# Block transposes on VectorE and row-placing DMAs in place of PE transposes, in a two-layer attention kernel

## The chip, the cores and the metric

The kernel runs on one core of one Trainium2 chip. The metric is device time in microseconds (us). The engines are PE (TensorE: matmuls, with weight loads of their own as PEld), DVE (VectorE), ACT (ScalarE), POOL (GpSimd) and SP (SyncE), which here issues every DMA. Each engine works through its own queue in order. PE writes to PSUM[...].

## The reference

Four batches of 512 tokens with 320 features go through two layers. Each layer is a self-attention, a cross-attention to a context of 1601 rows of 192 features, and a gated feed-forward with inner width 1280. All is fp32. There are 20 heads of 16 features. Cut to what matters:

```python
def _attn(x, ctx, wq, wk, wv, wo, bo, heads):
    ...
    sim = jnp.einsum('bhid,bhjd->bhij', q, k) * scale
    a = jax.nn.softmax(sim, axis=-1)
    out = jnp.einsum('bhij,bhjd->bhid', a, v)
    out = out.transpose(0, 2, 1, 3).reshape(b, n, heads * dh)
    return out @ wo + bo
h1 = _ln(x, n1_g, n1_b)
x = _attn(h1, h1, q1, k1, v1, o1_w, o1_b, heads) + x
h2 = _ln(x, n2_g, n2_b)
x = _attn(h2, context, q2, k2, v2, o2_w, o2_b, heads) + x
h3 = _ln(x, n3_g, n3_b)
proj = h3 @ ff_w1 + ff_b1
a, g = jnp.split(proj, 2, axis=-1)
return a * jax.nn.gelu(g, approximate=False) @ ff_w2 + ff_b2 + x
```

The softmax of a query needs the maximum of its scores, and at the end a division by the sum of its exponentials.

## The kernel before

**Units.** Attention is cut into units of one batch and four heads: per layer 20 units of self-attention (4 batches x 5 groups of heads), then 20 of cross-attention, then 4 feed-forward units, one per batch. A unit's keys are taken in chunks of 128: `nch` is 4 in a self unit and 13 in a cross unit (the last of 65 keys). `main` (L854) walks over the chunks of one unit. A chunk is two rounds; `tick` (L327) counts them in `clock["round"]`.

**Slots.** The four heads of a unit lie in slots of 32 partitions. 16 rows of a slot hold the head's features; the row `AUG` of the slot is a row of ones in the keys and a row of zeros in the queries. So that an exponential needs no bias, the negated maximum of each query is put into that row: the score matmul then subtracts it. Per chunk and head there is one score matmul (`st`, L862, queries moving, keys as weights), one exponential on ACT (`pr`, L868), and in `values` (L875), one chunk later, one matmul of the values (`av`, L882), with a column of ones for the sum of the exponentials. ACT copies the result from PSUM (`vo`, L898) and POOL adds it to `u.o` (L899), which holds the outputs with queries along the free axis, 16 rows and the row of sums (row `DH` of each slot).

**Maxima.** The maxima are found a unit ahead: beside every two score matmuls of unit n run two matmuls `sps` (L713) of a unit to come, with queries as weights and keys moving, and DVE reduces each of them (L721). `max_pairs` (L694) lists them, `giver` (L1079) hands them out so that they are done by a given number of rounds before that unit's start; a pair is at hand three rounds after the queries and keys that it reads were made. In a cross unit partial maxima `pm` are reduced once more by `max_reduce` (L758), one chunk before the end. They are queries on partitions. `max_end` (L764), after the scores of the last chunk, turns them: four transposes on PE (`mps`, L768), into PSUM, and one DVE addition of the queries `u.q` gives `qT` (L772), which the next unit's scores read.

**Finish.** `add_finish` (L774) is called when a unit's last values are emitted, in the first chunk of the next unit. `divide` (L777): four PE transposes of `u.o` (`dps`, L780), a reciprocal of the sums (L784), a product into `on` (L789). After the fifth group of heads `turn` (L796) transposes `on` back in three sets of four (`aps`, L801), with an ACT copy each into `aT` (L802), and eight steps of `project` (L804, `ops`) multiply by the output weights and add to `x`.

**Order.** The program order is written out by hand, and each engine keeps it. What stands beside the chunks (projections of queries and keys, values, context, norms, finish) waits in `chains`, as steps with a cost in us of PE time, a due round and conditions (`add`, L286). `steps` (L331) takes from them after each chunk, by due round (`pick`, L295) and by a credit that `pace` (L309) fills; steps of cost `LIGHT` have no PE work and are rationed to one or two per chunk. [...]a ring of four, `ps_st`, for scores and values, and a ring of four, `ps_m`, for the maxima and for the steps' matmuls (`step_bank`, L271). So a step or a maximum takes the bank that DVE or ACT has to leave first.

**DMAs.** `dma` (L80) is SP's `dma_start`. At the start `load_x`, `load_self`, `load_out`, `load_bias`, `load_cross` and `load_ff` (L1130 to L1138) are called before anything else; then the first unit's maxima are made without other units beside them, and `max_end(first)` (L1159) ends the start.

Of the kernel before, what the change touches and what calls it, by code (L numbers as in the profile page):

```python
# [59 lines left out]
def kernel(ctx: ExitStack, tc: tile.TileContext, x, context, ws, out):  # L60
# [51 lines left out]
    for i in range(2):  # L112
        m = const.tile([P, NQ, HG, SLOT], F32, name=f"nmax{i}")
        nc.gpsimd.memset(m, 0.0)
        nmax.append(m)
# [173 lines left out]
    def late_by(n):  # L289

        if clock["tiles"] is None or chains[n][0][0][0] == LIGHT:
            return 0
        return 0 if (n in ALIKE) == clock["tiles"] else 3
# [232 lines left out]
    held = {}  # L526
# [18 lines left out]
    def add_proj(u):  # L545
# [3 lines left out]
        due = lead(u) - 4  # L549
# [85 lines left out]

        for part in range(parts):
            add(chain, (0.05 + 0.427 / parts,) * 3, lambda part=part: queries(part), due - 2)
# [56 lines left out]
    def max_pairs(u):  # L694
# [4 lines left out]
        nm = nmax[u.n % 2]  # L699
# [10 lines left out]
        def full_one(t, s, j):  # L710
# [9 lines left out]
            to = nm[:, t, j, AUG[j] : AUG[j] + 1] if ns == 1 else u.pm[:, t, j, s : s + 1]  # L720
# [37 lines left out]
    def max_reduce(u):  # L758
        nm = nmax[u.n % 2]
        if u.pm is not None:  # L760
            for js in (slice(0, 2), slice(2, 4)):
                nc.vector.tensor_reduce(nm[:, :, js, AUG[js.start]], u.pm[:, :, js, :], AX.X, ALU.max, negate=True)

    def max_end(u):  # L764
        nm = nmax[u.n % 2]
        ps = step_bank([P, N], "mps")
        for t in range(NQ):
            nc.tensor.transpose(  # L768
                ps[:, t * P : (t + 1) * P], nm[:, t, :, :].rearrange("p j s -> p (j s)"), ident
            )  # L770
        u.qT = two.tile([P, N], F32, tag="qT", name="qT")
        nc.vector.tensor_tensor(u.qT, ps, u.q, ALU.add)  # L772

    def add_finish(u):  # L774


        def divide():  # L777
            ps = step_bank([P, NQ * HG, SLOT], "dps")
            for t in range(NQ):
                nc.tensor.transpose(  # L780
                    ps[:, t * HG : (t + 1) * HG, :].rearrange("p j s -> p (j s)"), u.o[:, t * P : (t + 1) * P], ident
                )
            rd = two.tile([P, NQ * HG], F32, tag="rd", name="rd")
            nc.vector.reciprocal(rd, ps[:, :, DH])  # L784
            if u.g == 0:
                held["out"] = one.tile([P, NQ, D], F32, tag="on", name="on")
            u.on = held["out"]
            u.divided = clock["round"]
            nc.vector.tensor_tensor(  # L789
                u.on[:, :, u.g * GD : (u.g + 1) * GD].rearrange("p t (j d) -> p t j d", d=DH),  # L790
                ps[:, :, :DH].rearrange("p (t j) d -> p t j d", j=HG),
                rd.rearrange("p (t j o) -> p t j o", j=HG, o=1).to_broadcast([P, NQ, HG, DH]),
                ALU.mult,
            )

        def turn(k, at, n):  # L796
            if k == 0:
                held["outT"] = one.tile([P, 3, N], F32, tag="aT", name="aT")
            ps = step_bank([P, N], "aps")
            for t in range(NQ):  # L800
                nc.tensor.transpose(ps[:n, t * P : (t + 1) * P], u.on[:, t, at : at + n], ident)  # L801
            nc.scalar.copy(held["outT"][:n, k, :], ps[:n, :])  # L802

        def project(t, part):  # L804
            cols = slice(part * D // 2, (part + 1) * D // 2)
            ps = step_bank([P, 512], "ops")
            for k, at, n in DK:
                for f, m in tiles_of(P):
                    nc.tensor.matmul(  # L809
                        ps[f : f + m, : D // 2],  # L810
                        lhsT=held["outT"][:n, k, t * P + f : t * P + f + m],
# [5 lines left out]

        r = clock["round"]
        add("divide", 0.58, divide, r + 6, yes, lambda: clock["round"] >= r + 2)
        if u.g == G - 1:  # L820
            for k, at, n in DK:
                add(
                    "divide", 0.58, lambda k=k, at=at, n=n: turn(k, at, n), r + 8 + k,
                    lambda: not chains["project"],
                    lambda: clock["round"] > u.divided,
                )

            def end():
                now = clock["round"]
                for t in range(NQ):  # L830
                    for part in range(2):
                        add(
                            "project", (0.317,) * 3, lambda t=t, part=part: project(t, part),
                            now + 6 + u.nch * t + u.nch // 2 * part,
                        )
                add("project", 0.0, lambda: after(u), now + 6 + u.nch * NQ)

            add("divide", 0.0, end, r + 10)
# [15 lines left out]
    def main(u, give, nxt):  # L854
# [3 lines left out]
        def score(c, j, pool=ps_st, tag="st"):  # L858
# [4 lines left out]
                st[:r, :], lhsT=u.kT[rows, u.k0 + c * P : u.k0 + c * P + r], rhs=u.qT[rows, :], start=True, stop=True  # L863
# [11 lines left out]
        def values(c):  # L875
# [15 lines left out]
            if c == 0:  # L891
                u.o = two.tile([P, N], F32, tag="o", name="o")
# [10 lines left out]
        for c in range(u.nch):  # L903
# [19 lines left out]
            if not last and c == u.nch - 1:  # L923
                max_end(nxt)
# [10 lines left out]
            if not last and c == u.nch - 2:  # L935
                max_reduce(nxt)
# [7 lines left out]
    def add_norms(i):  # L944

        while norms and norms[0].i <= i + (1 if norms[0].kind == "ff" else 5):
# [3 lines left out]
            else:  # L950
# [4 lines left out]
                due = lead(u) - 8  # L955
# [123 lines left out]
    def giver(u):  # L1079
# [14 lines left out]
        def give(h, alone=False):  # L1094
# [6 lines left out]
            for v in ahead:  # L1101
# [3 lines left out]
                rest = v.start - (7 if alone else 2) - clock["round"]  # L1105
# [5 lines left out]
            while owed >= 1.0 and any(left(v) for v in ahead) and not (alone and rounds and rest > -4):  # L1111
                hand = [v for v in ahead if left(v) and all(q and at_hand(v, q) for q in v.pairs)]
                if not hand and ahead[0].start - 2 - clock["round"] > 1:
                    break
# [92 lines left out]
```

## Time and profile before

| | |
|---|---|
| median of 3 runs | 3355.0 us (3354.72 to 3355.11) |
| profiled execution, its own time | 3355.09 us |
| its span, first to last instruction | 3353.3 us |
| granted TensorE clock | 0.999 |
| PE / DVE / ACT / POOL busy | 99 / 60 / 61 / 45% |
| four transposes `mps`, `dps` each, 80 times | 52.7 and 52.3 us busy |
| `aps`, 192 transposes in 48 sets | 29.4 us busy |
| ACT copies `aT`, 48 | 27.6 us busy |

A group's line names the kernel's line, the engine, what is written and read, and the count; then its busy time in us, the mean length of one in ns, and the idle time of the engine just ahead of it, with what ended it. Busy time is the union of the group's stretches; several matmuls on parts of the PE array run at once, so a group's busy time is less than count times mean. The ends of matmuls are modelled. A timeline line has the start and length in us. "SPq" is SP's queue: the time is that of issuing, and the landing is told apart. The self stages lie at about 30 to 435 and 1703 to 2110 us, the cross stages at 437 to 1400 and 2111 to 3066, the feed-forward between and after them.

### The profile page before, as it was taken

The page shows a single profiled execution, that of the slowest core. Times are in us where ns is not written, and L with a number is a line of the kernel's source. Part 1 is how long each engine was busy: PE and PEld are TensorE (multiplying, and loading weights), DVE is VectorE, ACT ScalarE, POOL GpSimd, SP SyncE. Part 2 cuts the span into 40 slices and gives each one's busy share as a digit, 9 for nine tenths or more (in the row PEclk, how much of TensorE's full clock was granted, in tenths as well). Part 3 has the DMA queues.
Part 4 walks back from the last instruction along what each step waited for, and adds up shares of the span by engine and source line. Part 5 has one row for each costly group of instructions (what it writes and reads, how often), then busy time and mean ns, then how long its engine had stood idle before and what let it go on. Part 6 is the DMA issues. An engine that isn't in the chain of part 4 may idle for free.

```text
span 3353.3 us, 81403 instructions
## 1 busy us (share of the span) xinstructions
PE 3315.3 (99%) x34386; PEld 1533.0 (46%) x34386; DVE 2025.8 (60%) x3724; ACT 2062.3 (61%) x4239; POOL 1519.6 (45%) x2252
## 2 busy tenths in 40 slices
PE   9999999999999999999999999999999999999999
PEld 4444444444444444355444444544444444443555
DVE  7666667767767666522256666677676676664221
ACT  5666467877877877711146664677777777776110
POOL 4544445645645654211225444456456556542000
PEclk9999999999999999999999999999999999999999
DMA  4001000100100000000020000000000000000000
GB/s 131 2 7 29 16 7 2 31 2 3 30 2 4 26 2 12 1 6 2 1 75 2 2 4 2 7 2 16 2 16 2 2 17 2 2 2 1 9 10 14
DMA packets 32117, 41.96 MB, mean 13 GB/s; under 512 B 11780, under 2 KB 30216, under 8 KB 30472
## 3 DMA queue, kind: packets, MB, share of 16 engines
q1 hardware_dynamic: 31752, 36.76, 3.9%
q8 instruction: 270, 4.42, 0.6%
q14 instruction: 95, 0.78, 0.1%
HBM read 29.21 MB, written 7.54 MB: 11 GB/s over the span
## 4 chain that ended last, share of the span: by engine, by line
PE 93%; DVE 5%; POOL 1%; ACT 1%; issue 1%; DMA 0%; SPq 0%; POOLq 0%; ACTq 0%; DVEq 0%
PE st L862 22%; PE av L882 19%; PE sps L713 15%; PE fps L984 8%; PE yps L1019 5%; PE kps L613 5%; PE vps L661 5%; PE ops L809 3%; PE qps L588 3%; PE fps L996 2%; DVE pm L721 2%; DVE nmax L721 2%; PE sps L728 2%; PE dps L780 1%; PE hps L422 1%; PE mps L768 1%
## 5 line engine op out<-in xcount | busy, mean ns | idle before, releaser
L868 ACT ACTIVATE pr<-st 128x512 f32<-128x512 f32 (+1 forms) x2720 | 1410.2, 601 | 559.9 <-PE sps L713 453.5
L721 DVE TENSOR_REDUCE pm<-sps 128x1 f32<-128x512 f32 x1920 | 1195.5, 683 | 498.3 <-PE sps L713 496.2
L862 PE MATMUL st<-qT,kT 32*128 32x512 f32 (+1 forms) x5440 | 1354.8, 614 | 22.1 <-DVE qT L772 10.1
L713 PE MATMUL sps<-kT,q 32*128 32x512 f32 x5120 | 1282.2, 617 | 2.3 <-ACT kst L630 1.5
L899 POOL TENSOR_TENSOR o<-o,vo 128x512 f32<-128x512 f32 x576 | 730.7, 1269 | 1124.2 <-ACT vo L898 1045.1
L882 PE MATMUL av<-pr,vals 128*32 128x512 f32 (+1 forms) x5440 | 729.3, 605 | 3.1 <-ACT pr L868 3.1
L862 PEld LDWEIGHTS st<-qT,kT 32*128 32x128 f32 (+1 forms) x5440 | 457.8, 181 | 275.5 <-ACT pr L868 96.4
L713 PEld LDWEIGHTS sps<-kT,q 32*128 32x128 f32 x5120 | 455.0, 183 | 243.6 <-issue 181.1
L721 DVE TENSOR_REDUCE nmax<-sps 128x1 f32<-128x512 f32 x640 | 397.0, 682 | 188.9 <-PE sps L713 188.0
L543 POOL TENSOR_SCALAR kT<-kst,keep,ones 64x200 f32<-64x200 f32 (+2 forms) x796 | 414.1, 520 | 88.9 <-ACT kst L623 31.5
L898 ACT COPY vo<-av 128x512 f32<-128x512 f32 x576 | 348.5, 605 | 47.6 <-PE av L882 47.2
L882 PEld LDWEIGHTS av<-pr,vals 128*32 128x32 f32 (+1 forms) x5440 | 109.8, 108 | 449.8 <-ACT pr L868 423.4
L984 PE MATMUL fps<-hT,w 128*128 128x512 f32 x640 | 288.2, 598 | 0.0
L1002 ACT ACTIVATE gl<-fps,b 128x512 f32<-128x512 f32 x80 | 54.8, 687 | 371.3 <-PE fps L996 371.3
L543 POOL TENSOR_SCALAR q<-qst,keep,zero 64x128 f32<-64x128 f32 (+1 forms) x476 | 230.0, 483 | 96.2 <-ACT qst L600 66.9
L984 PEld LDWEIGHTS fps<-hT,w 128*128 128x128 f32 x640 | 117.0, 190 | 141.7 <-issue 136.1
L661 PE MATMUL vps<-wv,ctxT 96*32 96x192 f32 (+2 forms) x3264 | 148.0, 299 | 0.0
L370 POOL TENSOR_SCALAR root<-root 128x4 f32<-128x4 f32 x23 | 5.3, 229 | 309.3 <-DVE root L364 308.8
L661 PEld LDWEIGHTS vps<-wv,ctxT 96*32 96x32 f32 (+1 forms) x3264 | 102.0, 109 | 94.3 <-issue 79.3
L669 ACT COPY vals<-vps 128x128 f32<-128x128 f32 (+3 forms) x272 | 82.4, 303 | 91.0 <-PE vps L661 87.4
L613 PE MATMUL kps<-ctxT,wk 96*32 96x200 f32 (+1 forms) x2560 | 136.9, 332 | 0.0
L1003 DVE SCALAR_TENSOR_TENSOR hid<-fps,b,gl 128x512 f32<-128x512 f32 x48 | 35.8, 750 | 155.1 <-ACT gl L1002 152.7
(83 smaller groups left out, 2465.6 us busy)
## 6 DMA issues: line engine op xcount, KB each, us to landing
ctxT<-ctxT SPq DMA_DIRECT2D x8, 1200.8 KB, 6.8
w<-in_L_xattn_ff_w_dram SPq DMA_DIRECT2D x4, 1280.0 KB, 9.2
ctxin<-in_ctx_dram SPq DMA_DIRECT2D x24, 192.0 KB, 2.6
w<-in_L_xattn_ff_w_dram SPq DMA_DIRECT2D x2, 1600.0 KB, 11.3
out_dram<-x SPq DMA_DIRECT2D x16, 160.0 KB, 1.8
x<-in_x_dram SPq DMA_DIRECT2D x3, 640.0 KB, 10.5
w1r<-in_L_xattn_ff_w_dram SPq DMA_DIRECT2D x4, 320.0 KB, 10.2
wq<-in_L_xattn_q_dram SPq DMA_DIRECT2D x8, 140.0 KB, 2.4
```

The lines of the kernel that those rows point to most:

```text
L543: nc.gpsimd.tensor_scalar(to, stage[rows, :w], keep[b][rows], more[rows], ALU.mult, ALU.add)
L613: nc.tensor.matmul(ps[to, :w], lhsT=wk[:n, k, gs], rhs=first.kvT[:n, k, c0 : c0 + w], start=(k == 0), stop=(k == len(u.kck) - 1),)
L661: nc.tensor.matmul(ps[f : f + m, at : at + w], lhsT=u.kvT[:n, k, c * P + f : c * P + f + m], rhs=wv[:n, k, h0 * DH : h1 * DH], start=(k == 0),
L713: nc.tensor.matmul(ps, lhsT=u.q[j * SLOT : (j + 1) * SLOT, t * P : (t + 1) * P], rhs=u.kT[j * SLOT : (j + 1) * SLOT, u.k0 + s * 512 : u.k0 ...
L721: return lambda: nc.vector.tensor_reduce(to, ps, AX.X, ALU.max, negate=(ns == 1))
L862: nc.tensor.matmul(st[:r, :], lhsT=u.kT[rows, u.k0 + c * P : u.k0 + c * P + r], rhs=u.qT[rows, :], start=True, stop=True)
L868: nc.scalar.activation(p[:r], st[:r], AF.Exp)
L882: nc.tensor.matmul(ps[i * SLOT : (i + 1) * SLOT, :], lhsT=columns_of[:r, head : head + SLOT], rhs=pr.pop((c, j))[:r, :], start=True, stop= ...
L898: nc.scalar.copy(vo, ps)
L899: nc.gpsimd.tensor_tensor(u.o, u.o, vo, ALU.add)
L984: nc.tensor.matmul(ps, lhsT=w1[:, k, i * FF + c * P : i * FF + (c + 1) * P], rhs=u.hT[:, k, :], start=(k == 0), stop=False,)
L1019: nc.tensor.matmul(ps[:, :D], lhsT=hid[c][:, t * P : (t + 1) * P], rhs=w2[:, c, :], start=(c == 0), stop=(c == NHC - 1),)
```

## The change

The maxima are written into 16 columns of a small tile `nm` [128, 32] in SBUF. `max_end` turns it on DVE as four squares of 32 by 32, so that each of 4 x 16 rows holds the maxima of 32 queries, and eight DMAs write these rows into the `AUG` rows of the queries `u.q` themselves: four for heads 0 and 1, four for heads 2 and 3, each of eight runs of 128 bytes. The scores read `u.q`; `qT` is gone. `max_reduce` and `max_end` are called one chunk earlier, and the maxima are due four rounds before a unit's start in place of two.

The finish is three steps: `sums` turns all 16 x 4 squares of `u.o` on DVE and takes the reciprocal, `divide` multiplies and turns back into `u.o`, and `turn` lets four DMAs put a unit's 4 x 16 rows into their place in `aT`. A projection comes at the earliest three rounds after the last `turn`. Since `u.q` is read by the scores until the unit ends, new queries wait until the unit that had the buffer is scored (`unread`). Queries, keys and norms are due two rounds sooner.

```diff
-        m = const.tile([P, NQ, HG, SLOT], F32, name=f"nmax{i}")
+        m = const.tile([P, SLOT], F32, name=f"nmax{i}")
...
-        if clock["tiles"] is None or chains[n][0][0][0] == LIGHT:
+        if clock["tiles"] is None or sum(chains[n][0][0]) < 0.1:
...
-        due = lead(u) - 4
+        due = lead(u) - 6
...
+        def unread():
+            return u.n < 3 or u.early or attn[u.n - 3].early or attn[u.n - 3].scored == attn[u.n - 3].nch
...
-            add(chain, (0.05 + 0.427 / parts,) * 3, lambda part=part: queries(part), due - 2)
+            add(chain, (0.05 + 0.427 / parts,) * 3, lambda part=part: queries(part), due - 2, unread)
...
     def max_reduce(u):
         if u.pm is not None:
-            for js in (slice(0, 2), slice(2, 4)):
-                nc.vector.tensor_reduce(nm[:, :, js, AUG[js.start]], u.pm[:, :, js, :], AX.X, ALU.max, negate=True)
+            nc.vector.tensor_reduce(
+                u.nm[:, : HG * NQ].rearrange("p (j t) -> p t j", t=NQ), u.pm, AX.X, ALU.max, negate=True
+            )

     def max_end(u):
-        ps = step_bank([P, N], "mps")
-        for t in range(NQ):
-            nc.tensor.transpose(
-                ps[:, t * P : (t + 1) * P], nm[:, t, :, :].rearrange("p j s -> p (j s)"), ident
-            )
-        u.qT = two.tile([P, N], F32, tag="qT", name="qT")
-        nc.vector.tensor_tensor(u.qT, ps, u.q, ALU.add)
+        turned = two.tile([P, SLOT], F32, tag="turned", name="turned")
+        nc.vector.transpose(turned, u.nm)
+        for half in range(2):
+            slots = u.q[half * GD : (half + 1) * GD, :].rearrange("(j s) n -> s j n", s=SLOT)[AUG[2 * half]]
+            for i in range(P // SLOT):
+                rows = slice(i * SLOT + half * 2 * NQ, i * SLOT + (half + 1) * 2 * NQ)
+                dma(
+                    out=slots.rearrange("j (t r) -> j t r", t=NQ)[:, :, i * SLOT : (i + 1) * SLOT],
+                    in_=turned[rows, :],
+                )
...
+        def sums():
+            nc.vector.transpose(turned.rearrange("p b s -> p (b s)"), u.o)
+            u.rd = two.tile([P, N // SLOT], F32, tag="rd", name="rd")
+            nc.vector.reciprocal(u.rd, turned[:, :, DH])
+            when.append(clock["round"])
+        def divide():
+            nc.vector.tensor_tensor(
+                turned[:, :, :DH], turned[:, :, :DH],
+                u.rd.rearrange("p (b o) -> p b o", o=1).to_broadcast([P, N // SLOT, DH]), ALU.mult,
+            )
+            nc.vector.transpose(u.o, turned.rearrange("p b s -> p (b s)"))
+            when.append(clock["round"])
+        def turn():
             if u.g == 0:
-                held["out"] = one.tile([P, NQ, D], F32, tag="on", name="on")
+                held["outT"] = two.tile([P, 3, N], F32, tag="aT", name="aT")
+            for j in range(HG):
+                f = u.g * GD + j * DH
+                k = next(k for k, at, n in DK if at <= f < at + n)
+                row = f - DK[k][1]
+                dma(out=held["outT"][row : row + DH, k, :], in_=u.o[j * SLOT : j * SLOT + DH, :])
+            if u.g == G - 1:
+                end(held["outT"])
...
-        add("divide", 0.58, divide, r + 6, yes, lambda: clock["round"] >= r + 2)
+        add("divide", LIGHT, sums, r - 20, yes, since(0, 2))
+        add("divide", LIGHT, divide, r - 20, yes, since(1, 1))
+        add("divide", 0.0, turn, r - 20, lambda: u.g or held["open"] < 2, since(2, 1))
...
-                rhs=u.qT[rows, :], start=True, stop=True
+                rhs=u.q[rows, :], start=True, stop=True
...
-                u.o = two.tile([P, N], F32, tag="o", name="o")
+                u.o = three.tile([P, N], F32, tag="o", name="o")
...
-            if not last and c == u.nch - 1:
+            if not last and c == u.nch - 2:
                 max_end(nxt)
...
-            if not last and c == u.nch - 2:
+            if not last and c == u.nch - 3:
                 max_reduce(nxt)
...
-                due = lead(u) - 8
+                due = lead(u) - 10
...
-                rest = v.start - (7 if alone else 2) - clock["round"]
+                rest = v.start - (7 if alone else 4) - clock["round"]
```

## The prediction

> **What bounds the kernel now.** I read the page's engine totals first, then the groups kept apart by form, then the timeline of one engine at a time around a boundary between two units. Columns of the first fence: busy us (share of the span) x instructions.
>
> ```profile
> PE 3315.3 (99%) x34386; PEld 1533.0 (46%) x34386; DVE 2025.8 (60%) x3724; ACT 2062.3 (61%) x4239; POOL 1519.6 (45%) x2252
> ```
>
> PE has 38 us of idle in 3353.3; no other engine is above 61%. So PE work that goes saves its own time, unless a new wait takes its place. The groups that the change removes (busy us, mean ns of one, idle before):
>
> ```profile
> L768 PE MATMUL mps<-ident,nmax 128*128 128x128 f32 x320 | 52.7, 287 | 0.3 <-DVE nmax L721 0.3
> L780 PE MATMUL dps<-ident,o 128*128 128x128 f32 x320 | 52.3, 286 | 2.6 <-POOL o L899 2.3 <-DVE pm L721 0.3
> L801 PE MATMUL aps<-ident,on 128*112 128x128 f32 x128 | 19.4, 282 | 0.0
> L772 DVE TENSOR_TENSOR qT<-mps,q 128x512 f32<-128x512 f32 x80 | 54.3, 679 | 6.8 <-PE mps L768 6.8
> ```
>
> Ends of matmuls are modelled, so I price a group of four transposes by starts. First an ordinary chunk of a cross unit, then the last chunk of one (PE timeline: start, length, what):
>
> ```profile
> 1007.42 0.70 PE L862 MATMUL st<-qT,kT 32*128 32x512 f32 x2
> ...
> 1009.35 1.07 PE L882 MATMUL av<-pr,vals 128*32 128x512 f32 x8
> 1010.23 0.86 PE L613 MATMUL kps<-ctxT,wk 96*32 96x200 f32 x16
> 1011.02 0.70 PE L862 MATMUL st<-qT,kT 32*128 32x512 f32 x2
> ```
>
> ```profile
> 1079.97 0.65 PE L862 MATMUL st<-qT,kT 32*65 32x512 f32 x2
> ...
> 1081.91 0.66 PE L768 MATMUL mps<-ident,nmax 128*128 128x128 f32 x4
> 1082.49 1.07 PE L882 MATMUL av<-pr,vals 128*32 128x512 f32 x8
> 1083.49 0.64 PE L501 MATMUL cps<-ident,ctxin 128*96 128x128 f32 x4
> 1084.39 0.70 PE L862 MATMUL st<-qT,kT 32*128 32x512 f32 x2 [0.25 <-DVE qT L772]
> ```
>
> Scores to values takes 1.93 us without mps and 2.52 with: a group costs 0.59. The ordinary chunk is 3.60 long, the boundary chunk 4.42: 0.59 of that is mps, the other 0.23 the wait for qT, which stands behind four reduces on DVE (2.48 us from 1081.16). Last, SP's queue at the start:
>
> ```profile
> 33.55 2.27 SPq L155 DMA_DIRECT2D w<-in_L_xattn_ff_w_dram  x2
> 35.86 1.11 SPq L199 DMA_DIRECT2D w1r<-in_L_xattn_ff_w_dram  x2
> 37.01 0.61 SPq L203 DMA_DIRECT2D w<-in_L_xattn_ff_w_dram  x1
> ```
>
> SP issues weights until 37.6 us, while PE starts its first scores at 30.27. In the DMA view of the first 40 us the last of these, 1600 KB, takes 15.0 us to land: 52.0.
>
> [...] No transpose of DVE is in this trace. [...] The additions from PSUM agree with such a rate: 160, 320 and 512 elements take 323, 492 and 679 ns, about 1 ns each plus 160. [...] Here the smallest loads (0.4 KB) land 2.0 us after issue, output stores 1.8.
>
> **The change part by part.** Price of a turn on DVE, not in the trace: 512 elements 0.69 us by the additions' line[...]. I take 0.69[...], and 0.2 for 32 elements.
>
> *Removed from PE:* mps and dps once in each of 80 units, aps three times in each of 16 batches and attentions: 208 groups x 0.59 = 122.7 us. With them go 48 ACT copies (27.6 us, off the path) and PSUM buffers that these shared with the maxima. The qT add goes too: its wait 0.23 x 38 cross boundaries = 9 us, and about 3 in the self stages: 12.
>
> *Added to DVE:* per unit two turns of 512 and one of 32 (1.58), against the qT add (0.68). Reciprocal (0.25) and product (0.42) stay; two reduces of 0.18 become one in a cross unit. Net some +0.8 us x 80 = 64 us on an engine at 60%. The finish comes as 0.94 (turn, reciprocal) in one chunk and 1.11 (product, turn) in the next. Behind them on DVE stand the next reduces, and for those PE waits, through the four PSUM buffers. What hides them is the idle between reduces: DVE works 2.48 of 3.60 us in an ordinary chunk, 1.1 free. Both fit; 5 us for coincidences with norm work. Without that cover they would cost their length.
>
> *Added to SP, maxima:* eight transfers of 1 KB per unit, four for heads 0 and 1, then four for heads 2 and 3. They are called one chunk before the old place. Clock from the start of chunk nch-2, cross stage: its last reduce ends at 3.44 in nearly all units, turn to 3.64, SP starts at 3.74. Issues in a row start 0.41 to 0.47 apart (four x loads in 1.81 us); at 0.46 the fourth is issued at 5.12 and the eighth at 6.96, and with 2.0 to land (range 1.6 to 2.4) they are there at 7.12 and 8.96. PE wants heads 0 and 1 at 3.64 + 3.60 = 7.24, so the first half is hidden, and heads 2 and 3 at 8.22 (0.98 into the chunk): 0.74 late. Four cross boundaries have longer chunks and room: 0.74 x 34 = 25. Self chunks are mostly 4.3 to 7 us: hidden except at a few dense boundaries, 8 in all. Behind the waiting score stand all of PE's matmuls, so a stall is paid in full.
>
> *Waits:* each half waits for four landings, up to eight more semaphore instructions of 0.05 us on PE's sequencer per unit (32 in all); most pass while matmuls run: 8.
>
> *Maxima due two rounds sooner, queries only once the unit three before is scored:* no work is added. In a self unit queries, keys and 16 maxima must now fit 12 rounds; I put it at 0, and the loss into the rivals' range.
>
> *Outputs:* four transfers per unit, 1.8 us of SP, with three rounds (6 us) before a projection reads them: hidden by that slack. SP in all: 12 x 80 x 0.46 = 442 us of 3353.
>
> *The start:* the first burst stands behind all start-up loads in SP's queue. Also, a transfer seems to wait for the one issued eight before it: x lands at 21.17 (9.2 after its issue at 11.97) and the eighth issue after it starts at 21.21; the next x lands at 22.94 and its eighth follower, a wq with nothing to do with x, starts at 22.97. Eight before the burst's last is the 1600 KB of w. So it starts at 52.0 and lands at 54.1; the scores of heads 2 and 3 of unit 0, at 31.2 before, wait for it: 23 us, with nothing else for PE. In mid-kernel the 1200 KB context transfers (6.8 us) may sit ahead of a burst once or twice: 5.
>
> Sum against the profiled span: 3353.3 - 122.7 - 12 + 23 + 25 + 8 + 8 + 5 + 5 = 3292.6. The profiled execution took 3355.09, 1.8 more than its span; the median of the three runs is 3355.0, so the same offset serves: 3294.
>
> **Rivals.** *All landings hidden.* If these transfers land in 1.6 us, the second half comes at 8.56 and the stall falls by more than half; with waits and coincidences at nothing I get 3250. For it: stores land in 1.8. Against: it needs every small term at its best.
>
> [...]
>
> *The burst on SP is dearer, and the kernel slower.* Some start-up issues took 0.6 us (w above, 0.61). At 0.65 an issue the eighth starts 1.33 us later: the cross stage stalls 2.1 at 34 boundaries, and about every self boundary by 0.9: 71 + 36 = 107 instead of 34, with the first half late too. That is 3368. It decides from about 0.61 us per issue, or as much in landing (3.1 us instead of 2.0).
>
> That the transposes stay is excluded: no line of mps, dps or aps is left; those of hps and cps are not touched.
>
> **How the numbers follow.** Forecast 0.52 (its own range 3265 to 3322), hidden 0.16, slow turns 0.16 (a fifth of it not faster), dearer burst 0.16. Faster by over 0.2% (6.7 us, about what this measurement can tell): 0.52 + 0.16 + 0.13 = 0.81; within 0.03; slower 0.16. The range 3243 to 3348 runs from the hidden case to the slow turns and leaves out most of the dearer burst.
>
> **What would show it.** Right: no mps, dps, aps on PE; PE's busy time near 3190; first scores of heads 2 and 3 near 54 us; PE idle before st released by DMA, 0.5 to 1 us at cross boundaries; turns of 0.69. Wrong: PE waiting on DVE's turns or reduces after a finish, starved maxima in the self stages, or bursts landing over 5.5 us after their turn.

## The result, and the profile after

The changed kernel takes 3387.8 us (median of 4 runs, 3386.79 to 3392.44) where the kernel before took 3354.86 (3353.26 to 3355.11): a ratio of 1.0102, 95% interval 1.0084 to 1.0119. It is slower by 33 us; the prediction was 3294 and its range ended at 3348. The profiled execution took 3392.44 us, its span is 3390.7, the granted clock 0.985 (0.999 before). It is the longest of the four, so the figures from its trace sum to 37 us more than before, not 33.

The page's engine totals of the kernel after:

```profile
PE 3263.5 (96%) x33554; PEld 1458.7 (43%) x33554; DVE 2092.3 (62%) x3844; ACT 2038.8 (60%) x4191; POOL 1526.0 (45%) x2252
```

832 transposes, 208 groups of four, are gone from PE, as the prediction counted (34386 - 33554), but its busy time fell by 52 us in place of 123, and its idle time rose from 38 to 127 us. The groups by form say what the new work on VectorE costs, and what PE waits for (columns as before):

```profile
L804 DVE STREAM_TRANSPOSE o<-oturn 128x512 f32<-128x512 f32 x80 | 56.9, 711 | 2.7
L794 DVE STREAM_TRANSPOSE oturn<-o 128x512 f32<-128x512 f32 x80 | 56.0, 701 | 25.9 <-POOL o L913 25.7
...
L772 DVE STREAM_TRANSPOSE turned<-nmax 128x32 f32<-128x32 f32 x80 | 16.1, 201 | 0.4 <-DVE nmax L764 0.4
```

```profile
L876 PE MATMUL st<-q,kT 32*128 32x512 f32 x5120 | 1315.2, 625 | 82.5 <-DMA q<-turned 55.1 <-ACT pr L882 12.6 <-DVE nmax L725 7.5
L717 PE MATMUL sps<-kT,q 32*128 32x512 f32 x5120 | 1305.4, 628 | 23.0 <-POOL kT L543 21.5 <-ACT kst L630 1.2 <-DVE kT L537 0.3
```

The turns are what was forecast (0.69 and 0.2 us). PE's new idle time has two names: the transfers into the queries' rows, 55.1 us (24.2 of them at the start), and POOL's writing of keys, 21.5 us, which is in no line of the kernel before. By stages, from the first scores of a stage to the first of its last unit or of the next stage; the forecast is the recorded sum split by where its groups and terms lie (of the 208 groups 96 lie in the self stages, 100 in the cross stages, 12 elsewhere; the small terms are halved):

| | before | after | forecast change | measured |
|---|---|---|---|---|
| start, to the first scores | 30.3 | 53.3 | +23 | +23 |
| self stages (two) | 406.9, 407.5 | 416.3, 412.6 | -43 | +15 |
| cross stages (two) | 933.5, 925.5 | 928.9, 935.9 | -34 | +6 |
| the rest | 649.8 | 643.7 | -6 | -6 |

So the start was right and both kinds of attention stage were off, by 57 and by 40 us.

**The start.** SP's queue and the first scores on PE:

```profile
37.77 0.59 SPq L203 DMA_DIRECT2D w<-in_L_xattn_ff_w_dram  x1
38.53 15.73 SPq L777 DMA_DIRECT2D q<-turned  x8
```

```profile
53.32 1.22 PE L876 MATMUL st<-q,kT 32*128 32x512 f32 x2 [24.24 <-DMA q<-turned]
```

The eight issues take 15.73 us. In the trace SP's transfers raise eight semaphores in turn, and the issue of the last one waits for the semaphore of the 1600 KB, issued eight before: those landed at 53.75 us, and it was issued at 53.77. But heads 0 and 1 waited nearly as long: their four transfers were issued by 45.2 us and landed only at 52.7 to 53.2, when the 1600 KB were nearly in.

**A cross boundary.** DVE, SP and PE around the start of the eleventh cross unit of layer 1 (start, length in us, what; in brackets idle before and its end):

```profile
2631.36 0.20 DVE L772 STREAM_TRANSPOSE turned<-nmax 128x32 f32<-128x32 f32 x1
```

```profile
2631.71 4.45 SPq L777 DMA_DIRECT2D q<-turned  x8
```

```profile
2635.06 0.70 PE L876 MATMUL st<-q,kT 32*128 32x512 f32 x2 [0.54 <-DMA q<-turned]
2635.07 0.70 PE L717 MATMUL sps<-kT,q 32*128 32x512 f32 x2
2635.57 0.62 PE L876 MATMUL st<-q,kT 32*128 32x512 f32 x2
2635.61 0.59 PE L717 MATMUL sps<-kT,q 32*128 32x512 f32 x2
2637.29 0.80 PE L876 MATMUL st<-q,kT 32*128 32x512 f32 x2 [1.09 <-ACT pr L882]
...
2637.82 1.12 PE L876 MATMUL st<-q,kT 32*128 32x512 f32 x2
...
2638.90 1.93 PE L896 MATMUL av<-pr,vals 65*32 65x512 f32 x8
```

Eight issues take 4.45 us, 0.56 each from start to start. PE waits 0.54 us for heads 0 and 1, and heads 2 and 3 start 2.23 us after them where 0.98 is the pace without a wait. (The bracket blames an exponential; but the last of the eight transfers landed at 2637.15, 0.14 us before these scores, and a run below shows that they can start without that exponential.) In 32 of 40 cross units this distance is over 1.5 us, mostly 2.1 to 2.3. After it the matmuls themselves are slow: values of 1.93 us where 1.07 is usual. The same place cut into windows (window; its length, then busy us and instructions of PE, PEld, DVE, ACT, POOL; granted clock; DMA share; GB/s):

```profile
2634.35:2637.76 3.41, 1.78 (x20) 0.68 (x16) 1.70 (x3) 1.64 (x4) 1.26 (x1) 1.00 0.01 2
2637.76:2641.17 3.41, 3.41 (x28) 0.93 (x24) 1.29 (x2) 1.35 (x3) 0.00 (x0) 0.50 0.02 5
2641.17:2644.58 3.41, 3.41 (x28) 1.29 (x20) 0.77 (x2) 1.44 (x4) 1.26 (x1) 0.50 0.00 0
2644.58:2648.00 3.42, 3.42 (x48) 1.58 (x48) 2.79 (x6) 2.31 (x6) 0.75 (x2) 1.00 0.01 2
```

Two waits of 1.6 us together, and then PE gets half its clock for 6.8 us. By the clock records there are 14 such stretches after, 99 us in all (the first, of 23.9 us at the start, has only 4.0 us of work in it); before there was one, of 3.4 us. PE is busy for 73 of the 99 us; by an estimate, half of that, some 36 us, is lost.

**A self unit.** PE and POOL in layer 0:

```profile
172.26 1.02 PE L876 MATMUL st<-q,kT 32*128 32x512 f32 x4
175.89 1.27 PE L717 MATMUL sps<-kT,q 32*128 32x512 f32 x4 [2.60 <-POOL kT L543]
177.09 1.94 PE L896 MATMUL av<-pr,vals 128*32 128x512 f32 x8
```

```profile
170.93 0.22 POOL L375 TENSOR_SCALAR root<-root 128x4 f32<-128x4 f32 x1
171.24 0.20 POOL L376 TENSOR_TENSOR root<-root,root 128x4 f32<-128x4 f32 x1
171.45 2.48 POOL L543 TENSOR_SCALAR q<-qst,keep,zero 64x256 f32<-64x256 f32 x4
174.03 2.47 POOL L543 TENSOR_SCALAR kT<-kst,keep,ones 64x256 f32<-64x256 f32 x4
```

POOL works through small steps of a norm (`root`), then spreads queries into slots, then keys, and PE stands in front of the maxima of these keys. In the kernel before the queries were made a chunk ahead of the keys; now `unread` holds them until the buffer's last reader, three units back, is scored, and both come in one chunk.

### The profile page after: what moved, and what is told of

The parts are those of the page before. It is cut to its first block, busy times and chain, and to the rows that moved or that the text cites. A ratio compares the mean times of both kernels' runs of the same rounds, so it can differ in the third digit from the quotient of the medians.

```text
span 3390.7 us, 82099 instructions
## 1 busy us (share of the span) xinstructions
PE 3263.5 (96%) x33554; PEld 1458.7 (43%) x33554; DVE 2092.3 (62%) x3844; ACT 2038.8 (60%) x4191; POOL 1526.0 (45%) x2252
## 5 line engine op out<-in xcount | busy, mean ns | idle before, releaser
L876 PE MATMUL st<-q,kT 32*128 32x512 f32 (+1 forms) x5440 | 1395.8, 623 | 86.5 <-DMA q<-turned 55.1
L717 PE MATMUL sps<-kT,q 32*128 32x512 f32 x5120 | 1305.4, 628 | 23.0 <-POOL kT L543 21.5
L896 PE MATMUL av<-pr,vals 128*32 128x512 f32 (+1 forms) x5440 | 740.2, 613 | 3.8 <-ACT pr L882 3.5
L876 PEld LDWEIGHTS st<-q,kT 32*128 32x128 f32 (+1 forms) x5440 | 471.3, 183 | 444.2 <-ACT pr L882 220.1
L717 PEld LDWEIGHTS sps<-kT,q 32*128 32x128 f32 x5120 | 441.3, 186 | 237.0 <-issue 143.5
L588 PE MATMUL qps<-hT,wq 112*32 112x128 f32 (+3 forms) x2880 | 127.7, 309 | 5.5 <-DVE nmax L725 3.9
```

The lines of the kernel that those rows point to most:

```text
L588: nc.tensor.matmul(ps[to, :w], lhsT=wq[:n, k, gs], rhs=first.hT[:n, k, at[i] : at[i] + w], start=(k == 0), stop=(k == 2),)
L717: nc.tensor.matmul(ps, lhsT=u.q[j * SLOT : (j + 1) * SLOT, t * P : (t + 1) * P], rhs=u.kT[j * SLOT : (j + 1) * SLOT, u.k0 + s * 512 : u.k0 ...
L876: nc.tensor.matmul(st[:r, :], lhsT=u.kT[rows, u.k0 + c * P : u.k0 + c * P + r], rhs=u.q[rows, :], start=True, stop=True)
L896: nc.tensor.matmul(ps[i * SLOT : (i + 1) * SLOT, :], lhsT=columns_of[:r, head : head + SLOT], rhs=pr.pop((c, j))[:r, :], start=True, stop= ...
```

## Experiments

Each line compares with runs of the kernel before on the same chip (medians 3352.9 to 3354.3 us).

| run | median us | ratio to before, 95% interval |
|---|---|---|
| finish alone | 3301.5 | 0.9843 (0.9828 to 0.9858) |
| maxima alone | 3430.4 | 1.0231 (1.0214 to 1.0248) |
| loads after the first burst | 3377.0 | 1.0067 (1.0052 to 1.0082) |
| four query buffers | 3365.6 | 1.0034 (1.0020 to 1.0047) |
| cross maxima a chunk sooner | 3336.2 | 0.9948 (0.9933 to 0.9963) |
| a matmul in the wait | 3394.0 | 1.0120 (1.0103 to 1.0137) |
| loads spread | 3376.4 | 1.0063 (1.0044 to 1.0081) |
| three repairs together | 3309.1 | 0.9869 (0.9854 to 0.9884) |
| both ways | 3305.7 | 0.9858 (0.9843 to 0.9872) |
| finish alone, two `aT` | 3293.6 | 0.9821 (0.9805 to 0.9838) |
| mix | 3290.3 | 0.9807 (0.9792 to 0.9822) |
| mix, sooner keys | 3275.7 | 0.9765 (0.9749 to 0.9782) |

### One half of the change at a time

The finish alone is the kernel before with `add_finish` of the changed kernel (`sums`, `divide`, `turn`), and for want of room one buffer `aT`; against the changed kernel's lines:

```diff
-                held["outT"] = two.tile([P, 3, N], F32, tag="aT", name="aT")
+                held["outT"] = one.tile([P, 3, N], F32, tag="aT", name="aT")
...
-        add("divide", 0.0, turn, r - 20, lambda: u.g or held["open"] < 2, since(2, 1))
+        add("divide", 0.0, turn, r - 20, lambda: u.g or held["open"] < 1, since(2, 1))
```

The maxima alone are the changed kernel with `add_finish` of the kernel before (`dps`, `aps` on PE).

> The kernel before with only the finish changed: sums, divide and turn on DVE and by DMA; the maxima stay on PE, with qT and the old due rounds. One aT buffer in place of two, for room. Theory (the loss lies in the maxima's half: start, boundaries, queries that wait): the finish keeps its whole saving, 80 x 0.59 for dps and 48 x 0.59 for aps = 75 us, so about 3280 us and a PE clock near 0.999. Rival (the turns of 0.7 us on DVE delay the reduces, and PE through the PSUM buffers): above 3310.

> The changed kernel with the finish of before (dps, aps on PE). Theory: it lacks the finish's saving of 75 us and keeps all losses: 3388 + 75 = 3463 us. Rival (the finish's half shares in the losses): the sum of the two halves' differences from before would not come to the +33 of both together; this one stays below 3435.

The finish alone gains 53 us and the maxima alone lose 76; together they should cost 23, and the changed kernel costs 33, so 10 come from their meeting: the maxima alone stayed under 3435 us, as their rival said, for the halves don't simply add. The rest of the loss is on the maxima's side. The finish gains, though less than its 128 groups x 0.59 = 75.5, and lies between its two forecasts. One wait of this run, on PE's timeline, looked like the cause:

```profile
283.09 1.12 PE L868 MATMUL st<-qT,kT 32*128 32x512 f32 x2 [2.77 <-ACT o L899]
284.14 1.94 PE L888 MATMUL av<-pr,vals 128*32 128x512 f32 x8
```

`u.o` was waited for, which the turns' DMAs hold while the single `aT` is in use (ACT's copy into `u.o` had waited 5.95 us for `aT<-o`). Values of 1.94 us again follow. This is tested at the end.

### The loads at the start

First behind the first unit's burst, in a second run spread over the units 1 to 6:

```diff
-    load_cross(0)
-    load_ff(0)
...
     max_end(first)
+    load_cross(0)
+    load_ff(0)
```

```diff
+    early_loads = {
+        1: lambda: load_cross(0),
+        2: lambda: (load_norm(0, 2), load_b1()),
+        3: lambda: load_w1(0),
+        4: lambda: load_w1(1),
...
     def before(u):
+        if u.i in early_loads:
+            early_loads[u.i]()
```

> The changed kernel with load_cross(0) and load_ff(0) called after max_end(first), so that the first burst does not stand behind 4.8 MB of weights. Theory: the 24.6 us gap at 53 us goes, and with it the half clock that follows it (12.7 us at half speed, some 6 us): 3388 - 30 = 3358 us; the first burst lands near 31 us. Rival (PE would be held there by the other loads in the queue anyway): less than 15 us gained.

> The changed kernel with the loads of the cross stage's and feed-forward's weights taken out of the start and spread over the start of units 1 to 6, the 1600 KB of w1 in two parts, so that no burst stands behind all of them. Theory (the 23 us at the start are SP's queue and the transfer eight ahead; with the loads apart each delays one burst by 1 or 2 us at most, in self units that have room): first scores near 31 us from 53.3, and 3360 us from 3387.8. Rival (the wait moves to the units whose bursts follow a load, as when all were put behind the first burst): 3372 or more.

In both the first scores come at 32.1 us, so the 23 us at the start were the loads ahead of the burst. But only 11 us are left of the gain in either, and both come out on the side of the rival. SP's and PE's timelines of the first of the two:

```profile
48.29 0.59 SPq L203 DMA_DIRECT2D w<-in_L_xattn_ff_w_dram  x1
57.03 7.73 SPq L777 DMA_DIRECT2D q<-turned  x8
```

```profile
63.79 2.07 PE L876 MATMUL st<-q,kT 32*128 32x512 f32 x4 [3.15 <-DMA q<-turned]
```

The next burst meets the same 1600 KB and is stretched to 7.73 us; unit 0 takes 31.7 us where it took 27.2. Spread out, each load costs a later burst little (the eight issues at 74.8 and 93.7 us take 4.38 and 4.47), but in the profiled execution the half clock is met oftener (17 stretches against 14; PE is busy for 86 us in them, against 73), and the self stages become 2.8 and 5.3 us longer. Where those stretches come from one by one is not settled, and they differ between executions: the four of this run take 3365.2 to 3380.5 us, at clocks of 0.992 to 0.986, and the profiled one is the longest.

### Four query buffers

```diff
-            return u.n < 3 or u.early or attn[u.n - 3].early or attn[u.n - 3].scored == attn[u.n - 3].nch
+            return u.n < 4 or u.early or attn[u.n - 4].early or attn[u.n - 4].scored == attn[u.n - 4].nch
...
-        u.qbuf = qbuf[3 if u.early else i % 3]
+        u.qbuf = qbuf[4 if u.early else i % 4]
```

> The changed kernel with four query buffers in turn in place of three, so that new queries wait for the unit four before, not three. Theory: in the self stages queries and keys need no longer crowd into the last chunk of a unit, the waits of 3 to 6 us for keys behind POOL's queue and the half clock after them go: about 12 us per self stage, 3362 us. Rival (it is the maxima's due round, two rounds sooner, that crowds them; keys have the same condition anyway): no change within 5 us.

The time is near the theory's: 22 us. The self stages fall from 416.3 and 412.6 to 409.6 and 403.7. What PE's maxima waited for (us, times), in this run:

```profile
L717 PE MATMUL sps<-kT,q x5120: 587/587/1217, 17.7 to 3038.6; 32*128 32x512 f32 x197
its engine sat idle before it (us, times) until:
  POOL kT L543: 5.9, 2
```

after 21.5 us in 8 times. The half-clock stretches at 177, 272, 395 and 1849 us, each of which began in or just after one of those waits, are gone with them: 58.0 us in all against 99.0. But PE is no less idle:

```profile
PE 3236.8 (96%) x33554; PEld 1444.4 (43%) x33554; DVE 2095.4 (62%) x3844; ACT 2041.1 (61%) x4191; POOL 1528.0 (45%) x2252
```

Of the span of 3363.8 us it stands still for 127, as in the changed kernel. Queries and keys lie apart again on POOL, and other waits have come in at the self boundaries: heads 2 and 3 start more than 1.3 us after heads 0 and 1 in 19 of the 40 self units, in place of 5, and the waits for the transfers rise from 55.1 to 61.2 us. So the theory holds for the cause, but what the run gains is mostly the clock: PE is busy at half clock for 38.9 us in place of 73, some 17 us less lost. Of the 26.9 us between the two profiled executions 15.6 lie in the self stages, where the theory had 24; the rest lies mostly in the cross stages.

### The maxima of cross units one chunk sooner

```diff
-            if not last and c == u.nch - 2:
+            if not last and c == u.nch - (3 if nxt.cross else 2):
                 max_end(nxt)
...
-            if not last and c == u.nch - 3:
+            if not last and c == u.nch - (4 if nxt.cross else 3):
                 max_reduce(nxt)
...
-                rest = v.start - (7 if alone else 4) - clock["round"]
+                rest = v.start - (7 if alone else 6 if v.cross else 4) - clock["round"]
```

> The changed kernel with the maxima of cross units reduced and sent one chunk (two rounds, about 3.6 us) sooner, and due two rounds sooner. Theory (heads 2 and 3 come some 1.15 us late at about 36 cross boundaries because the last of eight issues on SP starts 3.95 us after the first, and PE runs at half its clock after some of these waits): both halves are landed when PE wants them, 41 us of waits go, and some of the clock with them: about 3335 us from 3387.8, at the outside 3350; units in the cross stages start 0.9 to 1.3 us sooner each. Rival (the waits are not what costs in the cross stages, or the earlier maxima starve in turn): less than 20 us gained, over 3368.

3336.2, where the theory said 3335. The same boundary, SP and PE:

```profile
2600.37 4.45 SPq L777 DMA_DIRECT2D q<-turned  x8
```

```profile
2606.47 0.70 PE L876 MATMUL st<-q,kT 32*128 32x512 f32 x2
...
2607.45 0.59 PE L876 MATMUL st<-q,kT 32*128 32x512 f32 x2
...
2608.41 1.07 PE L896 MATMUL av<-pr,vals 65*32 65x512 f32 x8
```

The burst is as long as before, it only starts sooner; heads 2 and 3 follow at 0.98. The exponential that the bracket named is no sooner for it: it starts 1.16 us after the first scores here, 1.13 before, so these scores never needed it. PE's waits for these transfers are down to 25.3 us in 3 times, of which the start is nearly all. The cross stages become 915.1 and 893.4 us, 56 less in sum. Half-clock stretches in them went from 37.5 us to 6.8, worth 15; the waits themselves were 42 (29.1 us put down to the transfers, 12.6 to the exponential).

### A matmul in the wait

```diff
                     if odd:
                         tick()
+                    if c == 0 and odd and u.cross:
+                        warm(1)
```

> The changed kernel with one matmul more in the first chunk of every cross unit, on PE between the scores of heads 0 and 1 and those of heads 2 and 3: 128x128 by 512 columns, 0.85 us, into a PSUM bank that nothing reads (so it computes the reference and something unused beside). It stands where PE waits 1.15 us for the second half of the burst. Theory (waits themselves bring the half clock that this trace shows a dozen times): the matmul takes up most of the wait, costs next to nothing in time, and the half-clock stretches in the cross stages go: about 3375 us, 13 less. Rival (the clock has nothing to do with these waits): 3388 to 3400, as many stretches at half clock as before.

The time is the rival's, the clock the theory's. PE in this run, at the same boundary:

```profile
2640.90 0.62 PE L876 MATMUL st<-q,kT 32*128 32x512 f32 x2
...
2641.46 1.12 PE L281 MATMUL wps<-q,ident 128*128 128x512 f32 x2
2642.63 0.70 PE L876 MATMUL st<-q,kT 32*128 32x512 f32 x2
```

The matmul (it shows as two, x2, as the 2720 score matmuls show as 5440) fills the wait, heads 2 and 3 start 2.24 us after heads 0 and 1 as before, and no half clock follows: this unit takes 48.95 us in place of 52.20. In the cross stages 6 stretches of 37.5 us altogether became 2 of 10.2. But the distance is now at least 2.13 at the boundaries (a layer's last unit apart), also where there had been little to wait: up to the last cross units layer 0 loses 7 us, and layer 1 comes out even. So here waiting brought the half clock, and work in the wait mostly prevented it; it isn't a way to gain time.

### The repairs together

Four query buffers, the sooner cross maxima and the spread loads in one kernel:

> The changed kernel with four query buffers in turn, the maxima of cross units one chunk sooner, and the loads of the start spread over units 1 to 6: the three repairs together. Theory (their causes are apart: queries in the self stages -22 as run, cross boundaries -50, start -28): 3288 us, and the granted clock back above 0.995. Rival (they overlap, or PE meets another wait next: POOL, DVE or the bursts of the self units): over 3310.

They add up (-79 where the single runs sum to -85) and end 44 us below the kernel before; but neither 3288 nor better than the finish alone. The stages say why. The cross stages take 1812 us, 13 less than in the finish alone; the self stages take 817, 18 more. PE is idle there for 44 us in place of 31, and heads 2 and 3 start more than 1.3 us after heads 0 and 1 in 21 of the 40 self units (in none of the finish alone). That is a wait the rival had named, the bursts of the self units. The next two runs take from each side what had paid. Both ways, on top of four query buffers and the sooner cross maxima, with the loads where they were, with the dates of the kernel before for the self units, and, for room, one buffer each for the turned maxima and the turned outputs:

```diff
     def max_end(u):
+        if not u.cross:
+            ps = step_bank([P, N], "mps")
+            for t in range(NQ):
+                nc.tensor.transpose(
+                    ps[:, t * P : (t + 1) * P], u.nm[:, t, :, :].rearrange("p j s -> p (j s)"), ident
+                )
+            nc.vector.tensor_tensor(u.q, ps, u.q, ALU.add)
+            return
```

And the finish alone with two `aT`. Since the sum now goes into the queries themselves, it has four query buffers too, and one buffer for the turned outputs:

```diff
-        u.qT = two.tile([P, N], F32, tag="qT", name="qT")
-        nc.vector.tensor_tensor(u.qT, ps, u.q, ALU.add)
+        nc.vector.tensor_tensor(u.q, ps, u.q, ALU.add)
...
-                held["outT"] = one.tile([P, 3, N], F32, tag="aT", name="aT")
+                held["outT"] = two.tile([P, 3, N], F32, tag="aT", name="aT")
```

> A version that takes from each side what paid: the finish on VectorE and by DMAs as in the changed kernel; the maxima of cross units by VectorE and DMAs, one chunk sooner; the maxima of self units by four transposes on PE as before, the sum written into the queries in place; four query buffers in turn, the start as before. Theory (the losses are the burst at the start, the pressed queries of the self stages and the late second half in the cross stages, and nothing else): 3354.9 - 75 (128 groups of dps and aps) - 33 (40 of mps in the cross stages, with the qT wait) + about 12 of small waits = 3259 us, clock above 0.995. Rival (something else in the finish or the bursts costs, such as SP's time or DVE's): 3290 or more, no better than the finish alone.

> The kernel before with the finish alone on VectorE and by DMAs, as in the run of the finish alone, but with two buffers aT in place of one (room is made by adding the maxima into the queries in place and by one buffer for the turned outputs). Theory (the finish alone fell short of 75 us saved because the one aT held up the outputs, with waits of 3.4 us and half clock after them): 3285 us or less from 3301.5, half-clock stretches gone. Rival (the shortfall is DVE's or SP's work itself): within 5 us of 3301.

The second `aT`, with the buffers that came with it, was worth 8 us, a third of what was missing, so the run ends between its two theories. ACT's waits for `aT<-o` ahead of `u.o`, 7.5 us in 3 places, are gone. Its stages say where the rest is: the cross stages fall by 18.7 and 15.4 us, and 31 groups x 0.59 are 18.3; but the two self stages together fall by 19.7, where their 56 groups make 33.0. There PE's idle time rises from 18.8 to 27.9 us, and three half-clock stretches take 3.4 more than the one before: that is 12.5 of the 13.3 missing. So the groups give back nearly their price, and new waits and half clock take a part of it. Which waits these are is shown by no single line.

Both ways missed its 3259 by 47 us, and the theory with it; its rival was met. By units, the cross stage of layer 1 gained further (896.8 us against 910.1 in the finish alone with two `aT`), but the three self units before the cross stages took 88 and 93 us, against 79 and 80. PE there:

```profile
358.75 1.07 PE L909 MATMUL av<-pr,vals 128*32 128x512 f32 x8 [2.23 <-ACT pr L895]
359.63 3.90 PE L618 MATMUL kps<-ctxT,wk 96*32 96x200 f32 x48
...
372.07 1.14 PE L722 MATMUL sps<-kT,q 32*128 32x512 f32 x8 [1.54 <-POOL kT L548]
```

The keys of the first cross unit (`kps<-ctxT`) are pressed in as a block: its maxima are made beside self units of four chunks, and their date had moved two rounds forward with those of all cross units. And five cross units, four of them in layer 0, have two chunks of about 4.4 and 5.3 us with a crowd of the next unit's maxima in them. So two more runs; in the first (`mix`), the first cross unit of each layer goes by PE too, at its old time:

```diff
+        u.on_pe = not u.cross or u.early
...
-        if not u.cross:
+        if u.on_pe:
             ps = step_bank([P, N], "mps")
...
-                rest = v.start - (7 if alone else 6 if v.cross else 2) - clock["round"]
+                rest = v.start - (7 if alone else 2 if v.on_pe else 6) - clock["round"]
```

and in the second queries, keys, norms and context of the others come sooner as well:

```diff
-        due = lead(u) - (4 if u.on_pe else 6)
+        due = lead(u) - (4 if u.on_pe else 9)
...
-                due = lead(u) - (8 if u.on_pe else 10)
+                due = lead(u) - (8 if u.on_pe else 13)
```

> The run with both ways (finish by VectorE and DMAs; maxima by DMAs in the cross stages, by PE in the self stages), but with the first cross unit of each layer made by PE at its old time too, since its maxima are made beside self units of four chunks. Theory (what that run lost against its forecast of 3259 lies in the last three self units before the cross stage, 88 and 93 us where the finish alone has 79 and 80, because the first cross unit's maxima, queries and keys were due two rounds sooner there): both stretches shrink to about 80, 22 us go, 3284 us. Rival (they are long for another cause: POOL's queue or half clock): over 3298.

> The same, with queries, keys, norms and context of the other cross units due three rounds sooner than that. Theory (in five cross units, most of layer 0, the last maxima are made in one crowd of 29 and 19 matmuls in two chunks of 4.4 and 5.3 us in place of 3.5, since keys come too late for the sooner date; about 2.6 us each): 13 us less than the run beside it, about 3271 us. Rival (keys cannot come sooner, they wait for buffers or for the context): within 4 us of the run beside it.

Both went as the theories said, in sign and nearly in size: 15 us (22 expected) and another 15 (13). In the first the three self units take 80 and 78 us, and the self stages give 23; but the cross stages, whose first unit is now longer, give 9 back. The crowd, on DVE in the first of the two:

```profile
515.67 1.29 DVE L732 TENSOR_REDUCE pm<-sps 128x1 f32<-128x512 f32 x2 [1.09 <-PE sps L724]
516.87 0.76 DVE L749 TENSOR_REDUCE pm<-sps 128x4 f32<-128x260 f32 x2
519.81 2.48 DVE L732 TENSOR_REDUCE pm<-sps 128x1 f32<-128x512 f32 x4 [2.18 <-PE sps L724]
522.21 0.76 DVE L749 TENSOR_REDUCE pm<-sps 128x4 f32<-128x260 f32 x2
```

Two reduces of a unit's last 65 keys come on top of four ordinary ones, 3.2 us in a row, after DVE had stood still for 2.18. With the sooner dates this unit takes 46.67 us in place of 50.12, and those like it 45.0 in place of 47.6. The last run, 3275.7 us, is 78 us below the kernel before and 112 below the changed kernel: DVE and DMAs do the finish and the maxima of all cross units but the first of a layer, PE the maxima of the self units. Its PE is idle for 43 us:

```profile
PE 3232.5 (99%) x33722; PEld 1473.7 (45%) x33722; DVE 2119.8 (65%) x3846; ACT 2033.5 (62%) x4191; POOL 1525.4 (47%) x2253
```

## Why the prediction was wrong

**What held.** The bound: PE, and what is taken from it counts in its own time, in the cross stages nearly in full (18.7 and 15.4 of 18.3 us for the finish alone with two `aT`). The turns on DVE at 0.70 and 0.71 us, so the rival of slower turns falls. The wait of a transfer for the one issued eight before it. The start: +23, but in part by luck. The prediction let only heads 2 and 3 wait, for that last transfer; heads 0 and 1 waited nearly as long, for transfers that had been issued and didn't land. Heads 0 and 1 nearly on time at cross boundaries, heads 2 and 3 late. The chunk at the boundary without `mps` and the wait for `qT`: with the sooner maxima 3.58 us in many units, against 4.42, which is the 0.59 + 0.23 of the sum.

**"At 0.46 the fourth is issued at 5.12 and the eighth at 6.96 ... 0.74 x 34 = 25."** The term was right in kind and too small. An issue of these transfers takes 0.56 us, not the 0.41 to 0.47 of the x loads; the eighth starts 3.95 us after the first, not 3.22, and the first 0.2 later. The landing was shorter (1.6 us from the eighth issue to the scores, not 2.0), which gave a part back. The waits cost 42 us, 17 more than written.

**"Maxima due two rounds sooner, queries only once the unit three before is scored: no work is added ... I put it at 0."** This is the step that failed outright. No work was added, but two things that had stood in two chunks were put into one, behind a norm in POOL's queue: 21.5 us of waits on POOL, and half-clock stretches after them. The run with four buffers took 22 us back, though mostly through the clock. The loss was named as possible and left to "the rivals' range", where no rival held it.

**A term that wasn't there.** The sum took a wait at its length. In this kernel a wait costs more: PE is busy for 73 us at half clock, and of the 36 us lost 35 are new, nearly as much as the stalls of the cross stages. In the clock records of both traces the changes lie whole multiples of 3.41 us apart, and the stretches after the start are 3.41, 6.83 or 10.24 us, one, two or three times that. So I took PE's busy share of each window of this length, counted from a change of the clock. The window ahead of a stretch need not be idle: 1.78 busy of 3.41 us sufficed above. In the kernel before, after its start, the emptiest such window that wasn't followed by half clock is 0.70 busy, and the one that was is 0.51; after, 12 of the 14 that were lie between 0 and 0.60, though some of 0.50 to 0.60 went without. The other two were 0.80 and 0.94 busy; what brought the half clock there is open. The kernel before stays above this band but for that one window, and the two waits of 1.6 us together at the boundary above took theirs to 0.52.

**"208 groups x 0.59 = 122.7 us."** One price, taken from cross units, for every group. PE's busy time, with that at half clock counted half, fell by 87 us in place of 123: in the cross stages by 51 where 100 groups make 59, in the self stages by 29 where 96 make 57. About 4 us of the latter is work that moved: ten more steps of the cross units' values (`vps<-wv,ctxT`, 160 matmuls) stand in the self stages than before. Why the rest is missing stays open; in the finish alone with two `aT` the price nearly held (64 of 70 us in these stages).

**The accounts.** Each has three parts: PE's idle time, half clock, and what the groups fell short. Self stages, 57 us off: idle 13 (27 us more than before, 14 in the sum), half clock 17, groups 27. Cross stages, 40 off: idle 14 (39 against 25), half clock 18, groups 8. The whole profiled execution, 98 off: 27, 35 and 36. POOL's 21.5 us are within the idle time.

**The rivals.** The dearer burst ended nearest (3368), and its mechanism is the one of the cross stages; but its price of 0.65 us wasn't met, 0.56 is below its own threshold of 0.61, and alone it would have left the kernel faster. The sign came from the clock and from groups that gave less than their price, which stood in no case.

## What to carry to other kernels

When a step is given a new condition or an earlier date, lay out what then falls into one chunk on every engine's queue, down to the small steps of POOL; "no work is added" prices nothing. On an engine that is 99% busy, count a wait at its length plus what it may do to the clock (here PE's idle time came to 27 us more than in the sum, and half clock cost another 35), and look at the granted clock in narrow windows before and after. A change of two halves may hold a gain and a loss: here the half that has slack of several microseconds before its result is read paid, and the half whose result is wanted at once paid only where it was started a chunk sooner.

## What the runs showed of the hardware

- In the changed kernel, after its start, PE got half its clock after all windows of 3.41 us in which it was less than 0.50 busy, and after some of those up to 0.60, so not only after idle ones; two more stretches followed windows 0.80 and 0.94 busy. The 13 stretches lasted 3.41, 6.83 or 10.24 us.
- SP issued small transfers within SBUF (1 KB in eight runs of 128 bytes) every 0.56 us (eight in 4.45 us); at the cross boundary shown each half was read by PE 1.6 to 1.7 us after its last issue, the second some 5.7 us after the turn on DVE.
- In these programs SP's transfers raised eight semaphores in turn, and a transfer of 1 KB waited for one of 1600 KB issued eight before it: at the start of the changed kernel (15.73 us for eight issues) and again in the second unit's burst when the loads were moved (7.73). Four transfers issued in between landed late too, at 52.7 to 53.2 us after issues by 45.2.
- VectorE turned 128 x 512 fp32 in squares of 32 by 32 in 0.70 us and 128 x 32 in 0.20: by these two, about 1 ns for each of the 512 or 32 elements plus 0.17 us, near the 1 ns and 0.16 us of its additions (512 in 0.68).
